# Layer 1 of a two-layer graph kernel: product p3 in the inner level in turns with p7, the diagonal on ScalarE, and one table of places

## The chip, the cores and the metric

The kernel runs on one core of a Trainium2 chip. The metric is the time of one execution on the device in microseconds (us), lower is better. All times are of the whole kernel, for 16 batches and two layers.

## The reference

The input is x of 16 batches x 1024 nodes x 512 features, a 1024 x 1024 matrix adj, and the weights of two layers. All is float32.

```python
# layer 0
h = relu(layernorm(x))
x = x + (adj @ h) @ weight + bias
# layer 1
u = relu(layernorm(x))
h = u @ W
s1, s2 = h @ a[:512], h @ a[512:]
e = leaky_relu(s1[:, None] + s2[None, :], 0.2) * adj
att = softmax(e, axis=1)
x = x + elu(att @ h + beta * h)
```

Everything is per batch; only `adj` and the weights are shared. The time of layer 1 is in `att @ (u @ W)`, computed as `(att @ u) @ W`, where `att` differs from batch to batch and has to be made, transposed and combined on the other engines.

## The kernel before

**Products.** A matrix product of 1024 x 1024 by 1024 x 512 is done by a form of Strassen's method with seven products of half size, p1 to p7 (`PRODUCTS`). Each of the seven is 512 x 512 by 512 x 256. In the adjacency product of layer 1 the stationary operand comes from u (`ul_U`, `ul_S`) and the moving one from the transposed, not yet divided exponentials (`pT_..`, blocks B11 to B22 and the sums T1 to T4). A plain product (`plain_a`) is two halves of four matmuls, each 128 x 128 weights on 512 columns. The results gather in banks of PSUM that the trace calls z_Y, z_W and z_X; `ReadA` reads them, in part on ScalarE (copies) and in part on VectorE (sums), into the left operands of the second product (z_C, z_S).

The second product, with the weights W, is `Weighted`: again seven products, each of eight matmuls with 256 columns, into the banks pq_Y, pq_W and pq_X.

**The inner level.** `inner_steps` does one of the seven products by Strassen's method once more: seven steps r1 to r7 of two matmuls of 256 columns. For that it needs sums of the right operand (`block_sums`, three new tiles and one in place) and of the left one (`node_sums`), and extra copies and sums at the end. In layer 0 all seven products use it, from batch 1 on, since the right operands there are sums of adj that are made once. In layer 1 only p4 uses it (`p4_right`, `p4_left`), in turns with the first weighted product (`with_weighted`). p3 is plain there.

**Banks.** PSUM has six banks in one pool for z and pq, and two (`psum_y`) for the small results y and x of the inner level. pq's X banks are given those that z's Y banks leave, and these are free once VectorE has read the last steps of p4.

**Around the products.** While TensorE works on batch b, the other engines make the softmax of batch b+1: ScalarE writes leaky_relu(s1 + s2) (`masked`, Prelu), VectorE multiplies with the mask and takes the maximum, a trip through DRAM spreads the maximum over partitions (`spread_max`: md out, mall back), `top` makes it negative (nm), ScalarE takes exponentials with row sums (`exp`), VectorE transposes blocks of 32 x 32 (`turn`), a second trip spreads the sums (`spread_sum`), and `diagonal` adds beta times the row sum on the diagonal, which is beta * h in the reference. In batches 1 to 8 of layer 1 one further row of batch 15 of layer 0 is finished (`LateOut`: late in the trace). The outputs of the batch before are completed by an accumulating DMA on POOL's queue (o <- x1d), and stored from SP's queue.

**What sets the order.** Every engine's instructions keep the order in which the program records them: `InOrder` wraps all engines, which is why every row of the trace has line L119, the wrapper's own. What is recorded between which matmuls is written out by hand: `products_a` calls `after(k)` behind each half product or step, and plans say what is to be recorded at place k. For layer 1 there are several: `SOFTMAX_A`, `LATE_A`, `LATE_A2`, `LOADS_U` (lines 1202 to 1229) for places of the adjacency product, `SOFTMAX_B` and `LOGITS_B` for those of the weighted one, and `later`, into which `layer1` puts the ends of each output tile by counting places. In the plans M stands for `masked`, E for `exp`, V for `turn`, X and x for `spread_max`, N and n for `top`, S and s for `spread_sum`, D and d for `diagonal`, T1 to T4 for the block sums, U for loads and sums of u.

Of the kernel before, what the change touches and what calls it, by code (L numbers as in the profile page):

```python
# [61 lines left out]

A12_LATE = tuple(PRODUCTS[k] for k in (0, 3, 2, 1, 4, 5, 6))


@with_exitstack
def kernel(
# [128 lines left out]

    def inner_steps(name, prod, operands, read, banks, pl=b4, tag="b4"):

# [8 lines left out]
        y, x = yx[:, 0:256], (i0 if first else yx)[:, 256:512]  # L207
        t = pl.tile([P, 4, 256], F32, tag=tag, name=f"{name}_{prod}t")
        t5 = sums[:, 3].rearrange("p c d -> p (c d)")
# [15 lines left out]
        def step(r):  # L225
            o, start = outs[r]
            for k in range(2):
                pe.matmul(
                    o, lefts[r][:, k, :], rights[r][:, k, :], start=(start and k == 0),
                    stop=(k == 1), skip_group_check=True,  # L230
                )
            if r == "r1":
                act.copy(t[:, 0, :], y)
            elif r == "r5":
                act.copy(t5, x)
            elif r == "r6":
                if pl is b4:
                    add(t[:, 1, :], y, t5)
                else:
                    act.copy(t[:, 1, :], y)  # L240
                    add(t[:, 1, :], t[:, 1, :], t5)
            elif r == "r7":
                act.copy(t[:, 2, :], y)
                if first:
                    i0v = i0.rearrange("p (a n) -> p a n", a=2)
                    add(i0v, i0v, t[:, 2:3, :].to_broadcast([P, 2, 256]))
                else:
                    add(t[:, 3, :], t[:, 2, :], t5)
                    add(out(0), i0, t[:, 2:4, :].rearrange("p a n -> p (a n)"))
            elif r == "r3":  # L250
                add(out(1), i1, t[:, 0:2, :].rearrange("p a n -> p (a n)"))
# [3 lines left out]

        order = "r1 r4 r5 r2 r6 r3 r7" if first else "r1 r2 r5 r4 r6 r3 r7"
        return [partial(step, r) for r in order.split()]

# [15 lines left out]

    def products_a(name, a_blk, b_blk, after, products=PRODUCTS, s4=None, p4=None):


        banks = {}

        def fork(p):  # L280
            banks["W", p] = bank(f"{name}_W{p}")
            return banks["W", p]

        read = ReadA(name, fork if products is FORKED else None, s4)
        for n, (prod, an, bn, kind, first, last) in enumerate(products):
            if prod == "p4" and p4:
                inner, weighted = p4
                inn = inner_steps(name, prod, inner(), read, banks, ld, "ld")
                with_weighted(inn, read, weighted, lambda m: None, lambda m: after(2 * n + m))
                break  # L290
            for p in range(2):
                if first:
                    banks[kind, p] = bank(f"{name}_{kind}{p}")
                ps = banks[kind, p]
                plain_a(ps, p, partial(a_blk, an), partial(b_blk, bn), range(HC), first, last)
                read(prod, p, ps)
                after(2 * n + p)
        return read.left()
# [392 lines left out]
    class LateOut(LayerOut):  # L691


        def load(self, g):
# [5 lines left out]
            for i in range(2):  # L700
                sp.dma_start(out=self.v[:, i, :], in_=vd[i].partition_broadcast(P))
            self.norm = Norm(f"u{self.b}_{g}", self.u[:, 0:1, :])

        def stats(self):
            self.norm.stats()

# [35 lines left out]
    class Softmax:  # L742
# [33 lines left out]

        def masked(self, g):
            h, i = divmod(g, HC)
            if i == 0:
# [3 lines left out]
                }  # L783
            w = self.mask.pop(g)
            e = b4.tile([P, N], F32, tag="b4", name=f"e_{self.b}_{g}")
            for s in range(G):
                act.activation(
                    e[:, ts(s, SN)], self.s2b, AF.Prelu, bias=self.s1b[:, s, g : g + 1],
                    alpha=ALPHA,
                )  # L790
            for s in range(G):
                dve.tensor_tensor_reduce(
# [3 lines left out]
                )  # L796
            self.e[g] = e

# [58 lines left out]
        def diagonal(self, h):  # L857
# [5 lines left out]
            dve.reciprocal(self.rs[:, ts(h, HC)], sz[:, 0, :])  # L863
            dve.tensor_scalar(sz[:, 1, :], sz[:, 0, :], beta_c, None, op0=ALU.mult)
            for i in range(HC):
                d = self.t[f"B{h + 1}{h + 1}"][:, i, ts(i, P)]
                dve.scalar_tensor_tensor(
                    d, ident, sz[:, 1, i : i + 1], d, op0=ALU.mult, op1=ALU.add
                )

# [27 lines left out]
    def p4_left(b):  # L898
        p4_sums[b] = ld.tile([P, 4, 2, P], F32, tag="ld", name=f"in1_{b}")
        node_sums(partial(u_inner, b), p4_sums[b])  # L900

    def load_x1(b, nh, q):
        t = xp.tile([P, 2, D], F32, tag="xp", name=f"x1_{b}_{nh}_{q}")
# [5 lines left out]

    def layer1(b, plan_a, plan):  # L910

# [6 lines left out]
        def elu(nh, oh, q, z, k):  # L918
# [12 lines left out]
            def parts():  # L931
                for i in range(2):
                    sc = rs[:, g0 + i : g0 + i + 1]
                    act.activation(r[:, i, :], z[:, i, :], AF.Relu, scale=sc)
                    act.activation(ez[:, i, :], z[:, i, :], AF.Exp, scale=sc)

            if end or ez is not z:
                parts()
            else:
                later.setdefault(k + 1, []).append(parts)  # L940
            full = x1s[b, nh, q] if end else sums[nh, q]
# [17 lines left out]

            later.setdefault(k + (1 if end else 2 if ez is not z else 3), []).append(total)  # L960
            if nh != oh:
                later.setdefault(k + (1 if end else 7), []).append(store)

# [27 lines left out]
        def after(k):  # L991
            for f in later.pop(k, ()):
                f()
            beside(plan)(k)

# [3 lines left out]
        def p4_operands():  # L999
            return partial(u_inner, b), p4_sums.pop(b), pT["T4"], p4_ext.pop(b)  # L1000

        beside(plan_a)(-1)
        left = products_a(
            f"z{b}", lambda n, k: u_blk(b, n, k), lambda n, k: pT[n][:, k, :], beside(plan_a),
            FORKED, p4=(p4_operands, weighted1[0]),
        )
# [175 lines left out]
    def plan_softmax(order, s):  # L1182
# [3 lines left out]
            "S": [s.spread_sum, 0], "s": [s.spread_sum, 1],  # L1186
            "D": [s.diagonal, 0], "d": [s.diagonal, 1],
        }
        for g in range(NCH):
# [6 lines left out]
            names[f"R{g}"] = [s.reload, g]  # L1196
        for n in ("T1", "T2", "T3", "T4"):
            for k in range(2):
                names[n + "ab"[k]] = [s.right_sum, n, k]
        return {k: [tuple(names[n]) for n in steps.split()] for k, steps in order.items()}  # L1200

    SOFTMAX_A = {
        0: "M0 L4 M1 L5", 1: "M2 e6", 2: "M3 e7 X", 3: "M4", 4: "M5 M6", 5: "M7 x",
        6: "N B E0", 7: "E1 V0", 8: "E2 V1", 9: "n b E3 V2 S", 10: "E4 V3", 11: "E5 E6 V4",
        12: "E7 V5", 13: "V6 s", 15: "V7",
    }
    SOFTMAX_B = {1: "D", 2: "T1a", 3: "T1b", 4: "d", 5: "T2a", 6: "T2b"}
    LOGITS_B = {8: "L", 9: "L0", 10: "L1", 11: "e2", 12: "e3"}
    LATE_A = {5: "T3a T4a"}
    LATE_A2 = {6: "T3b T4b"}  # L1210


# [12 lines left out]
    FIRST_B = {  # L1225
        2: "E4 S R6", 3: "V4 E5 R7", 4: "V5 E6", 5: "D V6 E7", 6: "V7 s", 7: "T1a", 8: "T1b",
        11: "d T2a", 12: "T2b",
    }
    LOADS_U = {5: ("U00",), 7: ("U01",), 9: ("U10", "U11")}


# [45 lines left out]
    for nh, q in halves:  # L1277
        late.keep(nh, q)
        xrs.pop((B - 1, nh, q))
    w1_c = load_w("w1_c", w1)  # L1280
    for b in range(B):
        plans = [{
            k - 14: [(f,) for f in later.pop(k)] for k in sorted(later)
        }]
        plans.append(plan_softmax(LATE_A, sms[b]))
        late_a2 = plan_softmax(LATE_A2, sms[b])
        plans.append(steps((7, p4_right, b, 0), (8, p4_right, b, 1), (8, p4_left, b)))
        plans.append(steps((3, u_sums, b, 0, 1), (4, u_sums, b, 1, 1)))
        plan_b = {}
        if b == 0:  # L1290
            plans += [
                {7: [(w_sums, w1_c)]}, steps((-1, u_sums, b, 0, 0), (0, u_sums, b, 1, 0)),
            ]
        if b + 1 < B:
            plans.append(plan_softmax(SOFTMAX_A, sms[b + 1]))
            plans.append({k: [(load_u, b + 1, n)] for k, n in LOADS_U.items()})
            plan_b = plan_softmax(SOFTMAX_B, sms[b + 1])
        else:
            plans.append({7 + i: [(load_x1, b, nh, q)] for i, (nh, q) in enumerate(halves)})
        if b + 2 < B:  # L1300
            plan_b = merged(plan_b, plan_softmax(LOGITS_B, sms[b + 2]))
        if 1 <= b <= NCH:
            plan_b = merged(plan_b, {
                4: [(late.load, b - 1)], 9: [(late.stats,)], 10: [(late.relu,)],
                11: [(late.logits, b - 1)], 13: [(late.store,)],
            })
            if b == NCH:
                plan_b[13].append((late.store_logits,))
        if b + 1 < B:
            plan_b = merged(plan_b, steps((10, u_sums, b + 1, 0, 0), (12, u_sums, b + 1, 1, 0)))  # L1310
        plans.append({18: plan_b.pop(1, [])})
        layer1(b, merged(*plans, late_a2), plan_b)
    for k in sorted(later):
# [35 lines left out]
```

## Time and profile before

| | |
|---|---|
| time, median of 3 runs (lowest, highest) | 2247.63 us (2247.55, 2248.57) |
| span of the profiled execution, first to last instruction | 2245.6 us |
| the profiled execution's own time | not listed apart from the three runs; its span lies 2.0 us under their median |
| granted clock of TensorE | 0.998 |
| TensorE busy, matmul | 2229.6 us |
| VectorE busy | 1948.1 us |
| ScalarE busy | 1551.3 us |
| layer 1 | from about 1091 us of the span to its end |

The busy time of an engine is a sum over the whole span. A busy TensorE is not TensorE at its peak, since matmuls are pipelined and their ends are modelled: rows of matmul give 592 ns for one of 512 columns, while in a series they start further apart. The chain of waits, which adds up starts, is the better price. Idle time of an engine that isn't the bottleneck costs nothing in itself.

### The profile page before, as it was taken

How to read it: one execution, taken by the hardware profiler on the slowest of the kernel's cores; microseconds unless marked ns; L12 is line 12 of the kernel's file. 1: busy time of each engine (PE TensorE's matmuls, PEld its weight loads, DVE VectorE, ACT ScalarE, POOL GpSimd, SP SyncE). 2: the span in 40 equal slices, each digit the busy share in tenths (PEclk: the TensorE clock that was granted, in tenths of full speed). 3: DMA queues.
4: the chain of work that ended last, by engine and by line, in shares of the span. 5: the costliest groups of instructions: out<-in, count | busy, mean ns of one | idle time of the engine just before them, and what ended most of it. 6: DMA issues, size and time to landing. Idle time of an engine off the chain costs nothing.

```text
span 2245.6 us, 30403 instructions
## 1 busy us (share of the span) xinstructions
PE 2229.6 (99%) x8716; PEld 1648.6 (73%) x8716; DVE 1948.1 (87%) x4477; ACT 1551.3 (69%) x4138; POOL 245.0 (11%) x508
## 2 busy tenths in 40 slices
PE   9999999999999999999999999999999999999998
PEld 5788888888888888888666556665666556665565
DVE  7888898999898899889989988988889988898864
ACT  3776766676777677676566777767777776767743
POOL 1211111111111111111000000000000000000000
PEclk9999999999999999999999999999999999999999
DMA  6433454443444343345545665565654655546541
GB/s 207 145 127 120 159 172 133 140 145 120 142 160 164 130 149 122 105 151 184 191 116 161 169 176 155 153 188 157 167 176 141 191 148 149 140 141 166 159 119 50
DMA packets 194295, 336.06 MB, mean 150 GB/s; under 512 B 78800, under 2 KB 86992, under 8 KB 194128
## 3 DMA queue, kind: packets, MB, share of 16 engines
q1 hardware_dynamic: 185168, 302.15, 41.2%
q0 software_dynamic: 8640, 31.46, 7.5%
q8 instruction: 68, 1.11, 0.2%
q14 instruction: 99, 0.81, 0.1%
q10 hardware_dynamic: 320, 0.52, 0.1%
HBM read 228.33 MB, written 109.91 MB: 151 GB/s over the span
## 4 chain that ended last, share of the span: by engine, by line
PE 94%; DVE 3%; DMA 1%; ACT 1%; issue 0%; SPq 0%; POOL 0%; DVEq 0%; ACTq 0%; POOLq 0%
PE z_Y L119 15%; PE pq_Y L119 9%; PE po_Y L119 9%; PE z_X L119 9%; PE y_Y L119 8%; PE pq_X L119 5%; PE po_X L119 5%; PE z_W L119 5%; PE y_X L119 4%; PE y_W L119 3%; PE pq_W L119 2%; PE z_p4y L119 2%; PE po_W L119 2%; PE y_p3y L119 2%; PE y_p7y L119 2%; PE y_p4y L119 2%
## 5 line engine op out<-in xcount | busy, mean ns | idle before, releaser
L119 ACT ACTIVATE e<-e,nm 128x256 f32<-128x256 f32 x480 | 237.0, 497 | 47.0 <-DVE nm L119 47.0
L119 DVE CUSTOM_DVE_ANT_0 e<-e,mask 128x256 f32<-128x256 f32 x512 | 199.9, 423 | 54.2 <-ACT e L119 46.9
L119 PE MATMUL z_Y<-pT,ul_U 128*128 128x512 f32 x512 | 224.9, 592 | 0.0
L119 ACT ACTIVATE e<-s2b,s1b 128x256 f32<-128x256 f32 x512 | 214.7, 500 | 0.0
L119 PE MATMUL pq_Y<-w_c,z_C 128*128 128x256 f32 x768 | 189.1, 379 | 0.0
L119 PE MATMUL po_Y<-w_c,y_C 128*128 128x256 f32 x768 | 188.3, 379 | 0.0
L119 PEld LDWEIGHTS z_Y<-pT,ul_U 128*128 128x128 f32 x512 | 97.3, 190 | 115.6 <-issue 109.5
L119 DVE CUSTOM_DVE_ANT_0 y_S<-xr,v_bc 128x512 f32<-128x512 f32 x240 | 165.3, 689 | 8.9
L119 PEld LDWEIGHTS po_Y<-w_c,y_C 128*128 128x128 f32 x768 | 146.0, 190 | 20.2 <-ACT y_C L119 0.2
L119 PEld LDWEIGHTS pq_Y<-w_c,z_C 128*128 128x128 f32 x768 | 146.0, 190 | 19.8
L119 DVE STREAM_TRANSPOSE pT<-e 128x512 f32<-128x512 f32 x240 | 150.6, 680 | 0.0
L119 ACT ACTIVATE h<-h,nb_h,r_h 128x512 f32<-128x512 f32 (+1 forms) x132 | 98.2, 792 | 60.6 <-POOL nb_h L119 60.6
L119 ACT ACTIVATE y_S<-xr 128x512 f32<-128x512 f32 x90 | 56.7, 630 | 91.2 <-DVE xr L119 90.8
L119 POOL DMA_DIRECT2D o<-x1d x60 | 52.7, 935 | 609.7 <-DVE o L119 546.9
L119 PE MATMUL pq_X<-w_c,z_S 128*128 128x256 f32 x512 | 116.1, 380 | 0.1
L119 PE MATMUL po_X<-w_c,y_S 128*128 128x256 f32 x512 | 115.7, 379 | 0.0
L119 PE MATMUL z_W<-pT,ul_U 128*128 128x512 f32 x256 | 112.5, 592 | 0.0
L119 PE MATMUL z_X<-pT,ul_S 128*128 128x512 f32 x256 | 112.5, 592 | 0.0
L119 PE MATMUL z_Y<-pT_T,ul_S 128*128 128x512 f32 x256 | 112.5, 592 | 0.0
L119 PE MATMUL z_X<-pT_T,ul_S 128*128 128x512 f32 x256 | 112.5, 592 | 0.0
L119 PEld LDWEIGHTS pq_X<-w_c,z_S 128*128 128x128 f32 x512 | 96.5, 190 | 14.7 <-DVE z_C L119 1.2
L119 PEld LDWEIGHTS po_X<-w_c,y_S 128*128 128x128 f32 x512 | 97.3, 190 | 13.2
(259 smaller groups left out, 5236.7 us busy)
## 6 DMA issues: line engine op xcount, KB each, us to landing
mask<-maskd SPq DMA_DIRECT2D x128, 512.0 KB
h<-in_x_dram SPq DMA_DIRECT2D x64, 512.0 KB
xr<-in_x_dram SPq DMA_DIRECT2D x256, 128.0 KB
x1d<-xr SPq DMA_DIRECT2D x64, 512.0 KB
ul_U<-ud_U SPq DMA_DIRECT2D x64, 512.0 KB
ud_U<-xr SPq DMA_DIRECT2D x60, 512.0 KB
o<-x1d POOLq DMA_DIRECT2D x60, 512.0 KB, 8.3
out_dram<-o SPq DMA_DIRECT2D x240, 128.0 KB
```

The costliest lines, as they stand in the source:

```text
L119: return lambda *args, **kwargs: tc.keep_in_program_order(f(*args, **kwargs))
```

## The change

p3 of layer 1's adjacency product is now done in the inner level. Its seven steps stand in turns with the eight matmuls of p7, which come one by one (`TURNS`). Its right sums are made from B22 and its left sums from S4, in two more tiles of the pool b8. Its scratch is the tile that held the left sums, and its folded parts are added to C12 first, so that the banks of X are read as they are.

The diagonal is made as a product of the identity with the row sums on ScalarE (`dg`), and added by one VectorE instruction per half of the softmax. `LateOut` takes its mean and variance on ScalarE. Prelu is split off from `masked`.

The plans of layer 1 are replaced by one, `TABLE`, over all places of a batch: 0 to 7 are the halves of p1, p2, p6 and p5, 8 to 22 the turns of p7 and p3, 23 to 29 the steps of p4, and 30 to 41 the halves of the weighted products; -1 is ahead of the batch. Upper-case letters are as above; A is the Prelu, J the adding of the diagonal, r0, r1 and r the sums for p3, R0, R1 and R those for p4, and p, t and o with three digits the parts, the total and the store of one output tile.

```diff
+TURNS = "0 1 2 r 3 r 4 r 5 r 6 r 7 r r".split()
+TABLE_P4 = 8 + len(TURNS)
+TABLE_W = TABLE_P4 + 7
+TABLE = {
+    -1: "r0 o010 t100 T4a T3a", 0: "A0 t011 L4 B", 1: "L5 T4b U0b A1 A2 b U1b",
+    2: "M0 A3 M1 M2 A4 M3", 3: "T3b r A5 t101 L6 M4 X", 4: "M5 A6 A7 r1 M6 L7", 5: "o011 o100",
+    6: "N E0", 7: "o101 R M7", 8: "x E1 V0", 9: "R0", 11: "V1 E2", 12: "U00", 13: "R1 E3 V2",
+    15: "n", 16: "U01", 17: "V3", 19: "E4", 20: "E5 U10", 21: "V4", 22: "U11", 24: "E6", 26: "S",
+    27: "E7", 29: "D", 30: "L V5 Q0 s L0 L1 V6", 32: "J V7", 34: "U0a d t000", 35: "t001 T1a U1a",
+    36: "T1b j", 37: "Q1 p110 L2 T2a", 38: "L3 T2b", 39: "Q2 Q4 Q3 p111 p010", 40: "Q5 p011 t111",
+    41: "t110 t010",
+}
...
 # inner_steps, with a scratch tile given (fold)
             elif r == "r6":
-                if pl is b4:
+                if pl is b4 and not fold:
                     add(t[:, 1, :], y, t5)
                 else:
                     act.copy(t[:, 1, :], y)
                     add(t[:, 1, :], t[:, 1, :], t5)
+                if fold:
+                    c = read.block("C12", 1)
+                    add(c, c, t[:, 0:2, :].rearrange("p a n -> p (a n)"))
...
+                    high = t[:, 2:4, :].rearrange("p a n -> p (a n)")
+                    if fold:
+                        c = read.block("C12", 0)
+                        add(c, c, high)
+                        read(prod, 0, i0)
+                    else:
+                        add(out(0), i0, high)
+            elif r == "r3" and fold:
+                read(prod, 1, i1)
...
+        if fold:
+            order = "r1 r5 r4 r2 r6 r3 r7"
...
 # products_a
+            if prod == "p7" and p3:
+                inn = None
+                for m, turn in enumerate(TURNS):
+                    if turn == "r":
+                        if inn is None:
+                            operands, scratch = p3()
+                            inn = inner_steps(name, "p3", operands, read, banks, scratch=scratch)
+                        inn.pop(0)()
+                    else:
+                        p, k = divmod(int(turn), HC)
+                        plain_a(
+                            banks[kind, p], p, partial(a_blk, an), partial(b_blk, bn), (k,),
+                            first, last,
+                        )
+                        if k == HC - 1:
+                            read(prod, p, banks[kind, p])
+                    after(2 * n + m)
+                continue
...
 # diagonal
             for i in range(HC):
-                d = self.t[f"B{h + 1}{h + 1}"][:, i, ts(i, P)]
-                dve.scalar_tensor_tensor(
-                    d, ident, sz[:, 1, i : i + 1], d, op0=ALU.mult, op1=ALU.add
-                )
+                act.activation(dg[:, i, :], ident, AF.Copy, scale=sz[:, 1, i : i + 1])
+
+        def add_diagonal(self, h):
+            t = self.t[f"B{h + 1}{h + 1}"]
+            row = t.ap[0]
+            d = bass.AP(t.tensor, t.offset, [row, [HN + P, HC], [1, P]])
+            add(d, d, self.half[h]["dg"])
...
+    def p3_right(b, part):
+        if part == 0:
+            two = [
+                b8.tile([P, 4, 512], F32, tag="b8", name=f"in3_{b}_{i}") for i in range(2)
+            ]
...
+        block_sums(sms[b].t["B22"], p3_own[b][2], part)
...
+    def p3_left(b):
+        node_sums(partial(u_s4, b), p3_own[b][1])
...
 # LateOut
-            self.norm = Norm(f"u{self.b}_{g}", self.u[:, 0:1, :])
+            self.norm = Norm(f"u{self.b}_{g}", self.u[:, 0:1, :], self.u[:, 1, :])
...
-            self.norm.stats()
+            self.norm.sums(0)
```

## The prediction

> **What bounds the kernel now.** I read the busy time and the chain on the page first, then the busy times in windows of one batch of layer 1, then the chain and VectorE's timeline at the end of one batch.
>
> ```profile
> PE 2229.6 (99%) x8716; PEld 1648.6 (73%) x8716; DVE 1948.1 (87%) x4477; ACT 1551.3 (69%) x4138; POOL 245.0 (11%) x508
> ...
> PE 94%; DVE 3%; DMA 1%; ACT 1%; issue 0%; SPq 0%; POOL 0%; DVEq 0%; ACTq 0%; POOLq 0%
> ```
>
> TensorE carries 94% of the chain that ends last. The windows (core 0; PE, PEld, DVE, ACT, POOL busy) show the same batch by batch:
>
> ```profile
> 1091.00:1164.40 73.40, 72.41 (x239) 44.95 (x239) 66.73 (x162) 48.27 (x139) 0.00 (x0) 1.00 0.44 154
> ...
> 1450.10:1521.50 71.40, 71.40 (x237) 44.81 (x237) 63.32 (x158) 52.12 (x149) 5.32 (x8) 1.00 0.59 166
> ...
> 1878.90:1950.30 71.40, 71.40 (x237) 44.80 (x237) 61.42 (x151) 51.63 (x147) 3.48 (x4) 1.00 0.55 152
> ```
>
> A batch takes 71.4 us, and TensorE has no gap in it; VectorE is busy for 61.4 us, and for 63.3 us in the eight batches that also finish rows of batch 15 of layer 0. Batch 0 is the exception: 73.4 us, 1 us of it a TensorE gap, behind a VectorE that still has layer 0's last work. The price list of TensorE stands in the chain of waits:
>
> ```profile
> 1562.71 0.86 PE z_p4y L119 x4
> 1563.57 0.43 PE pq_Y L119 x2
> ...
> 1575.95 3.45 PE pq_W L119 x16
> ...
> 1593.22 6.87 PE z_Y L119 x16
> ```
>
> Counts hold weight load and matmul, so 8 matmuls of 512 columns take 6.87 us (0.858 each), and 8 of 256 take 3.45 us (0.432 each). A batch is six plain products, one inner product of 14 matmuls of 256 (p4), and seven weighted ones: 6 x 6.87 + 6.04 + 7 x 3.45 = 71.4.
>
> What could open a gap is the end of the p4 stretch, where VectorE releases z's Y banks to pq's X banks:
>
> ```profile
> 1494.40 4.86 DVE L119 STREAM_TRANSPOSE pT<-e 128x512 f32<-128x512 f32 x8
> 1499.18 0.38 DVE L119 TENSOR_TENSOR z_p4t<-z_p4t,in 128x256 f32<-128x256 f32 x1
> 1499.67 0.69 DVE L119 TENSOR_TENSOR z_C<-z_Y,z_p4t 128x512 f32<-128x512 f32 x1
> 1500.39 0.69 DVE L119 TENSOR_TENSOR z_S<-z_C,z_S 128x512 f32<-128x512 f32 x1
> ...
> 1501.45 0.69 DVE L119 TENSOR_TENSOR z_C<-z_Y,z_p4t 128x512 f32<-128x512 f32 x1
> ```
>
> This batch began at 1450.09; pq's first X matmul is due 41.20 + 9.49 = 50.7 us later, at 1500.8. The release at 1500.39 leaves 0.4 us. The waits say how near that is:
>
> ```profile
> PEld pq_X L119 <- DVE z_C L119: 1.2, 4, 0.5
> ```
>
> **The skill.** The Trainium skill, "TensorE: Matmul & The Clock Gate", table of specifications, says VectorE and ScalarE take their queue strictly first in, first out: one late operand holds all behind it. "VectorE: DVE Perf Modes", section on the TRN2 errata, gives an fp32 tensor_tensor (N+151)/0.96 ns, 692 for 512 columns; the rows have 691 to 692. In an unbroken row of them the timeline shows starts 0.60 apart where they are independent and 0.72 where one needs the one before; those I use. "DMA: Bandwidth & Descriptors", section on the anatomy of one DMA, puts a transfer's fixed cost at about 2 us; a small one (`md`) was issued at 1907.24 and its reader at 1909.30, so the trace agrees when the queues are quiet.
>
> **The change, part by part.**
>
> *p3 in the inner level.* 8 matmuls of 512 become 14 of 256: 6.87 - 6.04 = 0.82 us less per batch, all on TensorE's chain; 16 batches make 13.2 us. Layer 0 already runs this inner form at 0.432 us each, so I take no other bound. Turns with p7 only reorder: between two uses of the bank y lie at least 1.7 us, and its copy costs 0.37.
>
> *VectorE, added per batch.* Right sums, timed on p4's: 0.71 + 0.67 + 0.67 + 0.59 = 2.64. Left sums, 1482.75 to 1484.21: 1.46. The folds into C12: two of 256 at 0.45 and two of 512 at 0.72, 2.34. Diagonal: eight of 128 columns go (four start to end in 1.05, so 2.1) and two of 512 come (1.3). Sum +5.6. The late rows' statistics go to ScalarE (-1.05). VectorE then has 67.0 us of work, in batches 1 to 8 67.9, in a batch of 70.6. It fits, with 3 us to spare and no more; whether TensorE waits is a question of order.
>
> *ScalarE.* Four copies of 256 (0.37) and eight diagonal copies of 128 columns. No row shows the latter; from 0.2 (a 1-column activation) to 0.37 each; I take 0.3: +3.9 us on 52, plus 1.7 of statistics in eight batches. At 56 to 58 of 70.6 it is covered; its last exponentials stand before p4's copies, which then come at about +50.0.
>
> *The table.* Prelus leave `masked` and run up to two masks ahead, so VectorE's waits for ScalarE's e (46.9 us in all) should largely go. T3 and T4 move to the batch's start, five of the eight transposes stay ahead of p4's last adds, and the other three move behind them (3.6 us off the tight place). SP's queue keeps its transfers; twelve stores of finished tiles stand ahead of the second `md`, and the second row sums now behind the next logits (eight issues of 0.47, 3.8 us). The row sums are wanted 9 us after the last exponential, and SP, which waits for no matmul here, runs ahead: costed at nothing; without that cover VectorE would stand about 2 us at `diagonal`, where 5 us lie before TensorE needs anything from it. The mask loads stay one or two masks ahead of their use; a late one holds VectorE before N, where about 2 us are free. POOL's four accumulating DMAs spread over 20 us in place of 8, which I count for nothing either way. The b8 pool serves nine tiles per batch in place of seven from its ten buffers: the next batch's blocks take those of p1, p2 and p5's operands, read by +27.5, when its first transpose comes at about +29; if that read were late, the transpose would wait for it and no more.
>
> *The tight place again.* pq's X0 is now due at +49.86, X1 at +51.59 (40.37 + 9.49, and 1.73 later). I lay VectorE's list from its last unavoidable wait, the p3 rest at +67.1 of the batch before. Behind that stand: totals, p3's right sums, T3, T4, seven masks at 1.5, left sums, up to the first maximum (N): about +25. Left sums of p4 and mask 7 end at +28.5 to +29.4. Seven more us (p4's right sums, three transposes, a sum of C22) reach the second maximum (n) at about +36. From there: a transpose 1.22, the first fold 1.2, C22 0.6, p3's first read 2.66, a transpose 1.2, the second fold and read 3.83, then p4's 0.49 + 0.72. The first fold can't start before its matmul and copy (+38.4), so the first Y bank is free at about +49.0 to +49.3, the second at +51.2. Margins 0.6 and 0.4, as before; an error of 1 us either way in so long a sum is likely, so I charge 0.1 us to each of 15 batches, 1.5 us.
>
> *Batch 0.* VectorE has no slack here. It gains 6.4 us of p3 work ahead of the release, loses 3.6 of transposes and 0.8 of diagonal, and may lose 2.7 of waits for masks and e that the trace shows in it: from -0.7 to +2. I take +0.7: this batch gets no 0.82 and adds 0.7, 1.5 us off the gain.
>
> *The last batch.* Its tail of 9.6 us behind TensorE is unchanged; moved loads of x1 have 40 us to land. Costed at nothing.
>
> Sum: -13.2 + 1.5 + 1.5 = -10.2 us. The profiled execution has a span of 2245.6 and about 2.0 around it, if it ran like the median of 2247.63; taken from that, **2237.4**.
>
> **Rivals.** *All hidden:* every margin holds, batch 0 included: 2247.6 - 13.2 = 2234.4. For it: windows without a gap; against it: batch 0. *Given back:* VectorE comes 0.5 us later than my list (0.5 of 36 us is 1.4%), and each of 15 batches waits about 0.5: 2237.4 + 15 x 0.4 = 2243.4, at the edge of what can be told from no change. With 0.9, nothing is left. *Slower, by the second maximum:* VectorE stands at n until `md` has gone out and `mall` has come back, now with seven turns of 0.86 us between instead of four half products of 3.43. The waits on SP tell what can happen:
>
> ```profile
> SPq L119 <- DMA md<-mx: 139.3, 32, 8.5
> ```
>
> The mean is 4.35 us against the quiet 2.06. If the second pair meets the stores and an accumulating DMA ahead of it on SP and takes the mean, n is 2.3 us late, less 0.7 of margin makes 1.6 of stall, 15 x 1.6 is 24, and the time 2237.4 + 24 - 1.5 = 2260. It loses time as soon as n is 1.5 us late, and by over 0.2% at 1.8. Against it: in the trace twelve stores stood ahead of the second `md` and it still took 2.06. *The change isn't what it says:* the program of the changed kernel does issue 14 matmuls of 256 for p3; excluded.
>
> **How the numbers follow.** A measurement of this kernel can tell about 0.2%, 4.5 us: faster is below 2243.1, slower above 2252.1. My sum and the full cover have 0.70, both faster. Given back has 0.16 and lies between; slower has 0.14. The range takes my sum, the full cover and most of given back: 2233.2 to 2250.
>
> **What would show it.** Right: batches of 70.6 us in the chain, VectorE at 67 to 68 us in each window, X0 starting at +49.9, `pq_X <- DVE` among the waits with a few us at most. Wrong: batches of 71.4 or more, a line `DVE nm <- DMA mall` of 10 us or more, or TensorE gaps at pq_X of over 0.8 each; that would put the failure on the path through n or on VectorE's order.

## The result, and the profile after

| | before | after |
|---|---|---|
| time, median of 4 runs each (lowest, highest), us | 2247.76 (2247.55, 2248.57) | 2237.16 (2236.95, 2237.85) |
| ratio, 95% interval | | 0.995 (0.9936 to 0.9965) |
| profiled execution: span, own time, us | 2245.6, not listed apart | 2235.5, 2237.31 |
| TensorE clock granted, whole span | 0.998 | 0.998 |

The kernel became 10.6 us faster, 0.47%, and the forecast of 2237.4 lies within the runs. Whether its steps held is another matter, and half of what follows is about one that did not.

The page of the kernel after, busy times and the shares of the chain that ended last:

```profile
PE 2217.6 (99%) x8908; PEld 1684.6 (75%) x8908; DVE 2003.2 (90%) x4557; ACT 1614.9 (72%) x4370; POOL 246.1 (11%) x500
...
PE 92%; DVE 3%; DMA 2%; ACT 1%; issue 0%; SPq 0%; POOL 0%; DVEq 0%; ACTq 0%; POOLq 0%
```

TensorE has more instructions and 12 us less of work, VectorE has 55 us more. TensorE's share of the chain fell from 94 to 92%, and DMA's rose from 1 to 2%: somewhere TensorE waits that did not before.

The windows of the same three batches as before (PE, PEld, DVE, ACT, POOL busy, then clock, DMA share, GB/s):

```profile
1091.00:1166.34 75.34, 73.27 (x253) 48.46 (x252) 72.49 (x168) 52.81 (x155) 0.00 (x0) 0.98 0.48 158
1448.78:1519.39 70.61, 70.61 (x249) 47.03 (x249) 66.27 (x161) 56.89 (x166) 5.28 (x7) 1.00 0.59 168
1872.89:1943.50 70.61, 70.61 (x250) 47.03 (x249) 65.16 (x157) 54.67 (x159) 3.46 (x4) 1.00 0.55 153
```

A batch takes 70.61 us and TensorE fills it. Batch 0 doesn't: it is the only one with a clock below 1.00. From first matmul to first matmul, read from TensorE's timeline, batch 0 took 73.0 us before (the prediction's 73.4 is the length of its window) and takes 74.65 now; the others took 71.42 and take 70.61, but for one in each kernel (71.71 before; batch 9, 71.07, now). Batches are counted from 0. The sum: 15 x 0.81 = 12.2 less, 1.65 more in batch 0, about 0.2 for two odd batches and 0.3 for layer 0's end makes 10.1, the difference of the spans.

The tight place at the end of p4, VectorE's timeline in batch 11, whose first matmul starts at 1872.73:

```profile
1921.10 0.69 DVE L133 TENSOR_TENSOR z_C<-z_Y,z_p4t 128x512 f32<-128x512 f32 x1 [0.20 <-PE z_Y L133]
1921.82 0.69 DVE L133 TENSOR_TENSOR z_S<-z_C,z_S 128x512 f32<-128x512 f32 x1
...
1923.26 0.69 DVE L133 TENSOR_TENSOR z_C<-z_Y,z_p4t 128x512 f32<-128x512 f32 x1
```

The first Y bank is released at 1921.82, 49.1 us into the batch and 0.8 ahead of pq's first X matmul, which starts at 1922.62; VectorE itself waited 0.20 us for TensorE there, so it had time. The waits, which have no line of pq_X any more, show where the time went instead (PEld is the weight load, which overlaps the matmuls):

```profile
DVE nm L133 <- DMA mall<-md: 24.8, 14, 2.3
...
PEld z_p3y L133 <- ACT in L133: 10.0, 16, 2.9
...
PE z_p3y L133 <- ACT in L133: 2.3, 2, 2.1
```

TensorE waits for ScalarE at the bank y of p3 twice: 2.07 us in batch 0, and 0.19 in batch 9, the one that took 71.07. VectorE stands for the maximum's trip in 14 batches. Batch 0, TensorE's timeline, and under it ScalarE's in the same stretch:

```profile
1121.58 1.03 PE L133 MATMUL z_p3y<-pT,ul_S 128*128 128x256 f32 x4
1122.44 1.02 PE L133 MATMUL z_Y<-pT,ul_U 128*128 128x512 f32 x2
1125.53 1.95 PE L133 MATMUL z_p3y<-in,in 128*128 128x256 f32 x4 [2.07 <-ACT in L133]
1127.27 1.91 PE L133 MATMUL z_Y<-pT,ul_U 128*128 128x512 f32 x2
1128.98 1.10 PE L133 MATMUL z_X<-in,ul_S 128*128 128x256 f32 x4
1129.91 1.02 PE L133 MATMUL z_Y<-pT,ul_U 128*128 128x512 f32 x2
```

```profile
1120.22 0.59 ACT L133 COPY z_C<-z_X 128x512 f32<-128x512 f32 x1 [6.61 <-DVE mx L133]
1120.70 0.51 ACT L133 ACTIVATE e<-e,nm 128x256 f32<-128x256 f32 x1
...
1124.63 0.50 ACT L133 ACTIVATE e<-e,nm 128x256 f32<-128x256 f32 x1
...
1125.13 0.35 ACT L133 COPY in<-z_p3y 128x256 f32<-128x256 f32 x1
```

r1 leaves its result in the bank y, one p7 turn of 0.86 us follows, and r5 writes to the same bank; before that, ScalarE must have copied y. ScalarE keeps its order: the copy stands behind copies from z_X, and behind the eight exponentials of E0 and E1, which read VectorE's first maximum (nm). So r5 waited 2.07 us; then the matmuls up to 1129 ran at half speed (four in 1.95 in place of 1.03), which delayed the next ones by about 1.8 us. Together 3.9 of the 4.0 us by which batch 0 is longer than the others.

The 1.8 us are a delay at that place and not what the slow clock costs in the end. In the kernel with four further adds (below) batch 0 has the same instructions, and in its trace r5 waited as long, 2.06 us, with the clock at 1.00; TensorE then stood at p4, for VectorE and for ScalarE, and batch 0 took 74.12. By these two traces the slow clock is worth about 0.5 us; most of the rest would have been waited at p4.

### The profile page after: what moved, and what is told of

Read it like the earlier page. It is cut to its first block, busy times and chain, and to the rows that moved or that the text cites. A ratio compares the mean times of both kernels' runs of the same rounds, so it can differ in the third digit from the quotient of the medians.

```text
span 2235.5 us, 31175 instructions
## 1 busy us (share of the span) xinstructions
PE 2217.6 (99%) x8908; PEld 1684.6 (75%) x8908; DVE 2003.2 (90%) x4557; ACT 1614.9 (72%) x4370; POOL 246.1 (11%) x500
## 4 chain that ended last, share of the span: by engine, by line
PE 92%; DVE 3%; DMA 2%; ACT 1%; issue 0%; SPq 0%; POOL 0%; DVEq 0%; ACTq 0%; POOLq 0%
PE z_Y L133 15%; PE po_Y L133 9%; PE pq_Y L133 9%; PE y_Y L133 8%; PE z_X L133 6%; PE pq_X L133 5%; PE po_X L133 5%; PE y_X L133 4%; PE z_W L133 4%; PE y_W L133 3%; PE z_p4y L133 2%; PE pq_W L133 2%; PE z_p3y L133 2%; PE po_W L133 2%; PE y_p3y L133 2%; PE y_p7y L133 2%
## 5 line engine op out<-in xcount | busy, mean ns | idle before, releaser
L133 PE MATMUL z_Y<-pT,ul_U 128*128 128x512 f32 x512 | 238.9, 594 | 0.0
L133 DVE CUSTOM_DVE_ANT_0 e<-e,mask 128x256 f32<-128x256 f32 x512 | 182.0, 419 | 2.5 <-DMA mask<-maskd 2.4
L133 ACT ACTIVATE xr<-xr,nb_u,r_u 128x512 f32<-128x512 f32 x120 | 91.2, 808 | 19.0 <-POOL nb_u L133 19.0
```

The lines of the kernel that those rows point to most:

```text
L133: return lambda *args, **kwargs: tc.keep_in_program_order(f(*args, **kwargs))
```

## The experiments

The theories. **Theory 1:** the gain is TensorE's own work, 0.81 us per batch, and what limits the rest is VectorE's list, event by event. **Rival:** the gain comes from the table, the early Prelus and the diagonal, that is from waits taken off VectorE. For batch 0 there were two accounts of why ScalarE's copy is late: it stands behind mask 6 (part of theory 1 at first), or behind the first maximum (called theory 3 in the expectations, formed on the way). The last experiments are about these. All times are medians; the kernel before had medians of 2247.8 to 2248.5 beside them, and the intervals are of the ratio to it. The edits are shown shortened: "..." stands for what is left out, and the lines that allot or pass tiles are not shown.

### p3 plain again, all else kept

```diff
-inn = inner_steps(name, "p3", operands, read, banks, scratch=scratch)
-inn.pop(0)()
+inn = [[(1, 0)], [(1, 1)], [(1, 2)], [(1, 3)], [(0, 0), (0, 1)], [(0, 2)], [(0, 3)]]
 ...
+for p, k in inn.pop(0): plain_a(banks["X", p], p, ... "S4" ... "B22" ..., (k,), ...)
 ...
-"r0": (p3_right, b, 0), "r1": (p3_right, b, 1), "r": (p3_left, b),
```

> p3 is eight plain matmuls of 512 columns again, laid in the same seven places of the turns, without its sums and folds; table, early Prelus and ScalarE's diagonal stay. Theory 1 (the gain is TensorE's own work, 0.82 us in each batch): batches 1 to 15 go back to 71.4 us each, +12.3 us; batch 0 has no bank y of p3 to wait for and needs 73 to 74. Time 2247 to 2250. Rival (the gain comes from the table and the diagonal, which took waits from VectorE): batches stay at 70.6 to 70.9 and the time below 2241.

Measured 2246.03 (0.9983 to 0.9999). The chain at the start of two batches:

```profile
1163.69 6.87 PE z_Y L133 x16
...
1235.11 6.87 PE z_Y L133 x16
```

Batches are back at 71.42 us, as theory 1 has it; 15 x 0.81 of the gain is gone. The time lies 1 us under the range because batch 0 took 72.3 us: with p3 plain it has no bank y to wait for, and is 0.7 us shorter than before the change. So table, Prelus and diagonal together, with p3 plain, are worth about 1.8 us (the interval runs from 0.2 to 3.8), and p3's inner level costs batch 0 2.3.

### The diagonal on VectorE

```diff
-act.activation(dg[:, i, :], ident, AF.Copy, scale=sz[:, 1, i : i + 1])
 ...
-add(d, d, self.half[h]["dg"])
+dve.scalar_tensor_tensor(d_i, ident, sz[:, 1, i : i + 1], d_i, op0=ALU.mult, op1=ALU.add)   # x4
```

> The diagonal goes back to VectorE, eight instructions of 128 columns in place of two of 512 per batch, at the place where it was added; ScalarE loses eight copies of 128 columns (2.6 us). VectorE gets about 0.8 us more per batch, behind the tight place. Theory 1: nobody waits for that, batches stay at 70.6, 2236 to 2238.5; batch 0 may gain up to 1 us since VectorE no longer waits 1.34 us for ScalarE's tile. Rival (VectorE with 65 of 70.6 us is at its limit): 0.8 us in each of 15 batches, 2249.

Measured 2237.65 (0.9941 to 0.9966), within theory 1's range, but by two things that cancel. Batch 0 took 72.7 us, 1.9 less than with the diagonal on ScalarE. (Theory 1 had allowed it up to 1.) Batches 2 to 4 took 70.8 to 70.9, and 6 and 9 71.3: 0.8 us more on VectorE is not free everywhere. The place is the same as in batch 0: in batches 6 and 9 the first maximum starts 27.1 and 27.0 us into the batch, and r5 waits 0.46 and 0.45 us for ScalarE's copy. All of these are among batches 2 to 9, each of which begins behind the late row of the batch before. Neither theory had that.

### p7 whole, p3's steps behind it

```diff
-TURNS = "0 1 2 r 3 r 4 r 5 r 6 r 7 r r".split()
+TURNS = "0 1 2 3 4 5 6 7 r r r r r r r".split()
```

> p7 runs whole and p3's seven steps follow it back to back. Theory 1 (the turns give the copies of bank y their time): r5 comes straight behind r1 in the same bank and waits 0.5 to 0.8 us for ScalarE's copy, r7 behind r3 up to 0.5 more; the first fold comes 0.86 us later. 0.6 to 1.2 us in each of 16 batches, 2246 to 2256. Rival (the turns only reorder): 2236 to 2239, no wait at the bank.

Measured 2248.83 (0.9997 to 1.0014). The first line of the waits of TensorE's matmuls:

```profile
PE z_p3y L133 <- ACT in L133: 11.8, 17, 2.5
```

Batches take 71.32 us, 0.71 more each, in a wait for ScalarE at the bank y. Without a p7 turn between r1 and r5 the whole gain is gone. The turns are no mere reordering: they give the copy its 0.86 us, and not more.

### Four further adds on VectorE

```diff
 block_sums(sms[b].t["T4"], p4_ext[b], part)
+if part == 0 and b:
+    for _ in range(4):
+        add(spare, sms[b].t["T4"][:, 0, :], sms[b].t["T4"][:, 1, :])
```

> Four further adds of 512 columns on VectorE in each of batches 1 to 15, between the second trip of the maximum and the p4 stretch; nothing uses them. They cost VectorE 2.4 to 2.9 us per batch. Theory 1 (a gap opens when VectorE's list up to the release of Y is later than the margin): 1.4 to 2.2 us vanish in its waits there, 0.5 to 0.9 in the margin; 0 to 0.7 us per batch, 2237 to 2247, with a line of pq_X waiting for DVE. Rival (what counts is the sum, 65 of 70.6 us): it all fits, 2236 to 2238.

Measured 2248.84 (0.9995 to 1.0011), 1.8 over theory 1's range. Batches 2 to 9 took 71.6 to 72.6 us, 1 and 10 to 14 70.6 to 71.3. TensorE stands first at p4's first step into a Y bank, which VectorE reads for C22 (up to 0.67 us), and not at pq's X, where theory 1 had it: only the weight loads wait there, 0.3 us at most. VectorE's waits in batch 4, first with the adds (1381 to 1453), then those of the kernel after (1378 to 1448.6):

```profile
DVE nm L133 <- DMA mall<-md: 2.3, 1, 2.3
```

```profile
DVE nm L133 <- DMA mall<-md: 2.3, 1, 2.3
DVE in L133 <- ACT in L133: 0.5, 1, 0.5
DVE z L133 <- PE pq_Y L133: 0.3, 1, 0.3
DVE z_p4t L133 <- ACT z_p4t L133: 0.3, 1, 0.3
DVE z_C L133 <- PE z_Y L133: 0.2, 1, 0.2
```

What can give way are the small waits, 1.3 us; they are gone, and the wait for the maximum is as long as it was. 2.4 us of work (68.6 busy in a window of 72.0 us, 66.3 in one of 70.6 of the kernel after) less 1.3 leaves 1.1; these batches lost 1.0 to 2.0. VectorE has 4.3 us of idle time in batch 4 of the kernel after, and by this account, read in that batch alone, only 1.3 of it can be filled at that place.

### The same, with p4's left sums ahead of the maximum

```diff
-6: "N E0", 7: "o101 R M7",
+6: "R N E0", 7: "o101 M7",
```

> The kernel with four further adds per batch, with p4's left sums (1.46 us) ahead of the first maximum in place of behind it, so that they lie in the 1.8 to 2.2 us in which VectorE stands for the maximum's trip through DMA. Theory (with four more adds VectorE sets the pace, and its wait at the maximum is the only one left): batches 2 to 9 come from 71.9 down to 70.6 to 70.9, time 2237 to 2241. Rival (what counts is the work between the second maximum and the release of the Y banks, which is unchanged): 2247 to 2250 as with the four adds alone.

Measured 2247.55 (0.9987 to 1.0004): the rival's number. Its reason holds in part at most. VectorE's timeline in batch 4:

```profile
1407.60 0.26 DVE L133 TENSOR_REDUCE nm<-mall 128x16 f32<-128x64 f32 x1 [0.87 <-DMA mall<-md]
...
1408.90 0.42 DVE L133 CUSTOM_DVE_ANT_0 e<-e,mask 128x256 f32<-128x256 f32 x1 [0.83 <-DMA mask<-maskd]
```

SP's queue in that stretch:

```profile
1402.38 2.23 SPq L133 DMA_DIRECT2D mall<-md  x4
1404.65 0.47 SPq L133 DMA_DIRECT2D mask<-maskd  x1
```

The wait for the maximum shrank by 1.4 us as meant, and 0.8 came back at mask 7, whose load stands on SP behind the maximum's trip. That is 0.6 us gained of 1.4 in this batch. Batches 2 to 9 took 71.8 us on average in place of 72.1, and batch 0 lost 1.8 us more, since there the maximum came later. A wait that is filled shows the next one, on another queue. Loading mask 7 ahead of the trip wasn't tried, so it is not shown what the 1.4 us would have brought without it.

### Prelus back inside the masks

```diff
-0: "A0 t011 L4 B", 1: "L5 T4b U0b A1 A2 b U1b", 2: "M0 A3 M1 M2 A4 M3", ...
+0: "t011 L4 B", 1: "L5 T4b U0b b U1b", 2: "M0 M1 M2 M3", ...
```

> The early Prelus leave the table: ScalarE makes each mask's Prelu right before VectorE wants it, as before the change. Theory (VectorE's spare time in a batch is 1 to 1.6 us of waits other than the maximum's): some 2 to 3 us of waits for e come back, ahead of the first maximum, where nothing hides them; 0.5 to 1.5 us more in each of batches 1 to 8, 0 to 0.5 in the others; 2241 to 2250. Rival (65 of 70.6 us leaves room for 3 us of waits): 2236 to 2238.5.

Measured 2270.6 (1.0088 to 1.0122), far over both; the profiled execution is the fastest of the five, 2265.7. The waits of VectorE and of TensorE:

```profile
DVE e L133 <- ACT e L133: 45.3, 28, 2.5
...
PE z_p3y L133 <- ACT in L133: 21.2, 15, 3.5
```

The 2 to 3 us of waits for e came back, as said. They did not cost by way of the release of Y, where the expectation has them, but through the bank y: r5 waits in 15 of 16 batches. In ten of them the first maximum starts 25.8 us into the batch, without any wait for DMA, and r5 waits 0.80 us: here the Prelu of mask 7 (four activations, 1.6 us from the first start to the next instruction) stands between E0 and E1, ahead of the copy of y as well. These ten take 71.7 us; from batch 1 on four others take 73.2 to 75.1, with waits of 2.2 to 2.6 us at r5, and behind three of these four matmuls ran at half speed. With p3 plain, table, Prelus and diagonal were worth 1.8 us together; with p3 in the inner level the Prelus alone are worth 33.

### Batch 0: three sums moved

```diff
 if b == 0:
+    plans[0][-1].remove(r0); plans[0][4].remove(r1); plans[0][5] += [r0, r1]   # p3_right
-    plans += [{7: [(w_sums, w1_c)]}, ...]
+    plans += [{29: [(w_sums, w1_c)]}, ...]
-11: "d j T2a",
+10: "d", 11: "j T2a",
```

> In batch 0 of layer 1 alone, VectorE's list is rearranged: p3's right sums (3.3 us) go from places -1 and 4 to place 5, behind mask 6; the four sums of W1 (2.6 us) from place 7 to 29, behind the release of the Y banks; ScalarE's second diagonal one place earlier than the add that reads it. Theory 1 (batch 0 loses to ScalarE's copy of y, which stands behind a mask that VectorE makes late, and then to a TensorE clock of 0.54): both go, and VectorE reaches the release about 4 us earlier, so batch 0 takes 70.7 to 71.6 in place of 74.65, time 2233.5 to 2234.8. Rival (VectorE's sum of work bounds batch 0 whatever the order): another wait takes its place at the p4 stretch, and the time stays above 2236.

Measured 2239.88 (0.995 to 0.9975), slower than the change itself. Batch 0 took 75.5 us: r5 still waited 1.3 us, and pq's X products waited 3.05 us for the sums of W1, which I had put too late. So theory 1 was not tested by it; the rival (another wait takes the place) has it right, with the wait behind the p4 stretch and not in it. Batches 2, 3 and 6, whose instructions are the same, took 0.3 to 0.8 us more. In batches 3 and 6 it is r5 again (0.43 and 0.08 us), with the first maximum 27.0 and 26.7 us into the batch behind a wait of over 2 us for its trip; in batch 2 two later trips were late. Why a trip takes longer in one batch than in another stays open.

### Batch 0: right sums alone

```diff
 if b == 0:
+    plans[0][-1].remove(r0); plans[0][4].remove(r1); plans[0][5] += [r0, r1]   # p3_right
```

> The same with p3's right sums moved alone. Theory 1: the wait of p3's r5 for ScalarE's copy of y goes and the clock stays at 1.00, but VectorE's work up to the release of the Y banks is the same, 53 us without a pause in the trace, so TensorE waits there instead: batch 0 takes 72.9 to 73.9, time 2235.2 to 2236.4. Rival (only the bank y mattered): batch 0 at 70.7 to 71.4, 2233.5 to 2234.2.

Measured 2237.04 (0.9936 to 0.9963), no gain that can be told. Neither expectation holds. r5 waited 1.92 us still, although mask 6 was done 2.4 us earlier (at 1117.64 in place of 1120.06). VectorE's timeline says why:

```profile
1119.69 0.68 DVE L133 TENSOR_TENSOR pT<-pT 128x512 f32<-128x512 f32 x1
1120.29 0.25 DVE L133 TENSOR_REDUCE nm<-mall 128x16 f32<-128x64 f32 x1
```

The right sums now stand between mask 6 and the maximum, which is as late as it was, 28.5 us into the batch. From this came theory 3: what counts is the maximum, since E0 and E1 stand ahead of the copy. The clock stayed up behind this wait; TensorE stood 0.6 us more at p4, and batch 0 took 74.1.

### Batch 0: nothing ahead of the maximum; then two more steps

```diff
 if b == 0:
+    plans[0][-1].remove(r0); plans[0][4].remove(r1)            # all three
+    plans[0][7].remove(p4_left); plans[0][7] += [r0, r1, p4_left]
-11: "d j T2a", 12: "T2b",
+11: "d", 12: "j T2a T2b",                                     # second and third
-add(t1, b12, b11, ALU.subtract)  ... four sums of W1
+pool.tensor_tensor(t1, b12, b11, op=ALU.subtract)  ...        # third
```

> Batch 0 of layer 1 alone: p3's right sums and p4's left sums go behind mask 7, so that nothing stands between mask 6 and the first maximum on VectorE. Theory 3 (ScalarE's copy of y stands behind the eight exponentials of E0 and E1, and these behind VectorE's first maximum, at +28.5 us here and at +23.8 in the other batches): the maximum comes 2 us or more earlier, r5 waits at most 0.3 us in place of 2.0 and the clock stays at 1.00; then VectorE's list up to the release of the Y banks is late instead, by 1.5 to 2 us. Batch 0 takes 72.4 to 73.4 in place of 74.65, time 2235 to 2236. Rival (the copy stands behind mask 6 and the C22 copy): mask 6 is as early as in the kernel in which the right sums went behind mask 6, where r5 still waited 1.9; no change to that one, 74.1, 2237.

> The same, and ScalarE's last diagonal of batch 0 one place ahead of VectorE's add that reads it, so that an add of the residual (0.68 us) fills half of VectorE's 1.34 us wait for it. Theory 3: the list up to the release is 0.7 us shorter, batch 0 takes 71.7 to 72.7, time 2234.3 to 2235.3. Rival (something other than VectorE's list releases Y late): as without it, within 0.2 us.

> The same again, and the four sums of W1 on POOL, which is idle in batch 0, in place of VectorE (2.6 us). Theory 3: VectorE reaches the release 3.3 us earlier than in the first of the three, no wait is left: batch 0 takes 70.6 to 71.4, time 2233.2 to 2234.2. Rivals: POOL's four sums last over 20 us and pq's X products wait for them, as they did 3.0 us when VectorE made them behind the release (2236 or more); or POOL's work slows VectorE beside it, and some of the gain stays out.

Measured 2241.66, 2239.63 and 2240.72 (0.9962 to 0.9981; 0.9949 to 0.9974; 0.9954 to 0.9979): all three miss. Of the first, the maximum and TensorE:

```profile
1117.25 0.26 DVE L133 TENSOR_REDUCE nm<-mall 128x16 f32<-128x64 f32 x1
```

```profile
1137.45 2.07 PE L133 MATMUL z_Y<-pT_T,ul_U 128*128 128x256 f32 x4 [4.26 <-DVE z_C L133]
```

The account of the copy held: the maximum came at +25.9 in place of +28.5 and the 2.07 us at r5 were gone (in batch 9 of the same run r5 waited 0.7, the longest there). But what came next was larger than I said: TensorE stood 4.26 us at p4's first step into a Y bank, which VectorE reads for C22 first, and the clock dropped behind it. Batch 0: 76.7 us. VectorE's list bounds this batch, and the expectation had counted only its end. Of the 4.26 us, 1.5 are a wait of VectorE for the load of mask 7, which the earlier maximum laid open, as in the kernel with the sums ahead of it:

```profile
DVE e L133 <- DMA mask<-maskd: 1.5, 1, 1.5
```

The second kernel met the same gap (4.2 us): its wait at the diagonal was 0.6 shorter, and that for mask 7 0.4 longer.

The third took 2.6 us off VectorE. POOL made the four sums in 5.60 us (its timeline, first line), not the 20 I feared. But VectorE's masks beside it (second fence):

```profile
1107.92 5.60 POOL L133 TENSOR_TENSOR w_c<-w_c 128x512 f32<-128x512 f32 x4 [62.96 <-DMA w_c<-in_L_gnn_W_dram]
```

```profile
1107.73 0.42 DVE L133 CUSTOM_DVE_ANT_0 e<-e,mask 128x256 f32<-128x256 f32 x1
...
1108.07 1.49 DVE L133 CUSTOM_DVE_ANT_0 e<-e,mask 128x256 f32<-128x256 f32 x1
...
1109.49 1.48 DVE L133 CUSTOM_DVE_ANT_0 e<-e,mask 128x256 f32<-128x256 f32 x1
```

Four mask instructions took 1.48 us each in place of 0.42, as long as one POOL sum each. That is 4.3 us lost to save 2.6; the maximum came at +29.6 and r5 waited 3.1.

### Batch 0: the first softmax's diagonals on VectorE

```diff
 def diagonal(self, h):
+    if self.b == 0:
+        self.half[h]["sz"] = sz
+        return
 def add_diagonal(self, h):
+    if self.b == 0:
+        for i in range(HC): dve.scalar_tensor_tensor(d_i, ident, sz[:, 1, i : i + 1], d_i, ...)
+        return
```

> The diagonals of the first softmax of layer 1, made in the last batch of layer 0, go on VectorE (eight instructions of 128 columns), all others stay on ScalarE. Theory 3 (in batch 0 the first maximum on VectorE is the late event): VectorE no longer stands 1.34 us for ScalarE's tile right ahead of batch 0, the maximum comes at +27.0 in place of +28.5, r5 waits 0.5 us and the clock stays at 1.00; batch 0 takes 72.5 to 73.2, as where all diagonals were on VectorE (72.7), and the others 70.6; time 2234.9 to 2235.9. Rival (that kernel's short batch 0 came from ScalarE's lighter load within batch 0): batch 0 stays at 74 to 74.7, 2236.5 to 2237.4.

Measured 2235.49 (2234.97 to 2236.14; 0.993 to 0.9958). TensorE's timeline:

```profile
1124.14 1.13 PE L133 MATMUL z_p3y<-in,in 128*128 128x256 f32 x4 [0.52 <-ACT in L133]
```

Batch 0 took 72.6 us, the wait is 0.52, and the clock stayed. This version is the best of all by its median, 1.7 us under the change; that step alone (0.07%) is less than the intervals can tell, and rests on the reading of batch 0. The kernel with all diagonals on VectorE has the same batch 0 (72.7) and is 2.2 us slower; in its trace batches 2 to 9 lost 2.2 us against 70.61, in that of this kernel 0.5.

The runs line up, as far as p3's turns and ScalarE's list up to the copy are those of the kernel after. The first maximum's start, counted from the batch's first matmul, and r5's wait:

| kernel, batch 0 (else as named) | maximum at | r5 waits |
|---|---|---|
| nothing ahead of the maximum | +25.9 | none |
| after, batch 9 | +26.8 | 0.19 |
| all diagonals on VectorE | +27.0 | 0.50 |
| first diagonals on VectorE | +27.0 | 0.52 |
| all diagonals on VectorE, batch 6 | +27.1 | 0.46 |
| three sums moved | +27.9 | 1.33 |
| right sums moved | +28.5 | 1.92 |
| after | +28.5 | 2.07 |
| W1's sums on POOL | +29.6 | 3.11 |
| four adds, p4's left sums first | +30.0 | 3.4 |

Each microsecond of the maximum beyond about +26.5 is one of TensorE. In batches 1 and 10 to 14 of the kernel after, the maximum is at +23.9 to +24.4, its wait for DMA included: 2.1 us of margin or more. In batches 2 to 9 it is at +25.3 to +26.8, a margin of 1.2 us in the best of them and none in batch 9. So the steady batches that begin behind a late row stand at the same edge as batch 0, and a trip of the maximum that is late by a microsecond is enough.

## Why the prediction was right, and where it wasn't

- **p3, 0.82 us per batch:** measured 0.81 (71.42 to 70.61). Confirmed by taking p3 back: 71.42.
- **"Turns with p7 only reorder: between two uses of the bank y lie at least 1.7 us":** this step failed. Between r1 and r5, which write y and x in one bank, lies one turn of 0.86 us; 1.7 us are from the start of r1 to that of r5, and the copy can't begin before r1 is done. And the copy's price is not its own 0.37 us: it also has to wait for what stands ahead of it on ScalarE. In all of batches 1 to 15 but batch 9 it still fits; without turns it costs 0.71 us a batch, and in batch 0 it is where TensorE stood.
- **0.1 us for each of 15 batches (1.5):** not needed; the 0.46 us of batch 9 are r5's and not the release's. The release was seen at +49.1 where +49.0 to +49.3 was said, and X0 at +49.9 as said, so 0.8 of margin in place of 0.6.
- **Batch 0, +0.7:** measured +1.65, at another place. The range of -0.7 to +2 held; where TensorE stood was not the release to pq's X but p3's r5, and then came a stretch at half clock, which the prediction didn't have (about 0.5 us, by the two traces above). The two mis-sized terms, 1.3 too much and 1.0 too little, nearly cancel. That the total is so near is luck; that it is a gain of about 10 us is not, since it rests on p3's 0.81 us.
- **VectorE at 67.0 and 67.9 us:** measured 65.2 and 66.3; the sum of the parts is 1.6 to 1.8 too high. What made it safe was not this average: with 0.8 us more, batches 2, 3, 4, 6 and 9 were longer, and 2.4 us more cost the whole gain.
- **ScalarE at 56 to 58:** 54.7 and 56.9; four diagonal copies took 1.19 us to the start of the next instruction (1147.96 to 1149.15), 0.30 each, as was taken.
- **Prelus, "VectorE's waits for e should largely go":** 46.9 us before, and no such row is left after, only 2.4 us for mask loads. The 2 us of slack ahead of N are there in batches 1 and 10 to 14 (2.1 to 2.6), not in batches 2 to 9 (1.2 to none) nor in batch 0, and the prediction named no one who waits behind N. It is ScalarE's E0 and E1, and through them TensorE's r5.
- **The rivals:** "slower, by the second maximum" did not come: n had no wait over 0.1 us in any batch. It is the first maximum at which VectorE stands, 24.8 us in all, over the 10 us that the prediction had put down as a sign of failure; TensorE has no gap in 13 of these 14 batches, and 0.19 us in batch 9. "All hidden" failed at batch 0, and by half a microsecond at batch 9. "Given back" did not come. That "the change isn't what it says" is excluded by the counts as well.
- **A reading of the rows:** "counts hold weight load and matmul" is not so, and what stands ahead of the prediction on rows of 592 ns goes wrong with it. The chain's PE pieces hold matmuls alone; each matmul that the program writes leaves two rows. The rows of 512 columns start 0.43 us apart, closer than their 592 ns, and two of them make the 0.858 us. The sums are of whole products and stay as they are.
- **The Trainium skill**, "TensorE: Matmul & The Clock Gate", table of specifications, with its strict first in, first out on ScalarE, was cited for VectorE's late operands. The same sentence decides batch 0: eight exponentials stand ahead of one copy of 0.35 us, and the trace agrees (1120.70 to 1125.13 of the fence above). Two of the prediction's figures need a word: the formula gives 691 ns for 512 columns and not 692, and the section on one DMA is written for transfers that POOL issues, while `md` goes by SP; what counts is the 2.06 us of the trace.

## What to carry to other kernels

When an inner product is split into steps that share a small bank, look for the nearest two uses of that bank, and follow the copy between them back through the copying engine's whole queue to the last thing that it waits for. An average of idle time says little of what an engine can take on: count only the waits that would shrink if the work were put at that place, since a wait for a trip through DMA that starts only behind that place stays as long as it was. A kernel that just fits in every steady batch can lose in its first one, where the work of the stage before still stands in the queue; and the margin is to be read in the tightest of the steady batches, not in one of them.

## What the runs showed of the hardware that I had not expected

- **The clock after a gap.** In layer 1 the traces show nine stretches in which TensorE ran at half clock; each lasted 3.41 us, and one 6.83, twice that. The kernel with the late Prelus has four of them, and the second to the fourth begin 221.87, 655.36 and 730.45 us after the first, which is 65, 192 and 214 times 3.413. So there is a window of 3.413 us that runs on whatever the kernel does, and a stretch at half clock fills one window or two. Cut along these windows, the traces separate: behind a window at full clock in which TensorE was idle for 2.07 us or more (2.07 to 3.41, nine of them), the next one ran at half clock; behind one with 2.00 us or less, none did. The ends of matmuls are modelled, so the limit of about 2 us is no better than that. Two gaps of the same length at r5, of the kernel after (2.07) and of the one with four adds (2.06), in windows of TensorE (us, busy time, clock, DMA share, GB/s):

```profile
1122.29:1125.70 3.41, 1.34 (x5) 1.00 0.03 5
1125.70:1129.11 3.41, 3.41 (x7) 0.50 0.51 139
```

```profile
1120.71:1124.12 3.41, 2.62 (x9) 1.00 0.01 3
1124.12:1127.54 3.42, 2.15 (x8) 1.00 0.15 18
1127.54:1130.95 3.41, 3.41 (x14) 1.00 0.89 271
```

The first gap lies within one window. The second is split over two, 0.8 and 1.3 us, and the clock stays; so is the gap of 3.05 us in front of pq's X in the kernel with three sums moved (1.49 and 1.56). Where a window begins differs from run to run, so whether a gap of 2 to 4 us slows the clock is in part chance. The Trainium skill, "TensorE: Matmul & The Clock Gate", section on HAM oscillation, gives gaps over some 3.4 us as the ones to avoid; here 2.07 us were enough, and the measurement decides. That the window runs freely and lasts 3413 ns the same page states in its section "What's actually happening", and the traces agree.

- **POOL and VectorE.** A mask instruction of VectorE went from 0.42 to 1.48 us beside POOL's sums. The Trainium skill, "SBUF — State Buffer", section "Who interferes with whom", says that a VectorE instruction with two SBUF inputs contends with a GpSimd one that reads SBUF, and calls the ports that they share an exclusive lock; the mask instruction reads e and mask, and the trace agrees: each of four mask instructions took as long as one of POOL's sums (1.40 us).
